# A graph-attention and slice-attention layer on one core: compact slice attention, shared PSUM places, and a new order of work at both ends

## The chip, the core and the metric

The kernel runs on one core of one Trainium2 chip. Its five engines work side by side: TensorE (PE, with its weight loads shown as PEld), VectorE (DVE), ScalarE (ACT), GpSimd (POOL) and SyncE (SP), which here issues transfers. The metric is device time in microseconds. The kernel before takes 2727.98 us, the median of three runs from 2726.14 to 2728.41; the profiled execution spans 2730.5 us.

## The reference

Everything is float32. `x` is 32 batches of 512 rows and 256 features; `adj` is a sparse 512 x 512 mask. Two layers with residuals follow each other, each on layer-normalised input:

```python
def _gat(inp, adj_mask, W, a):
    h = inp @ W
    f1, f2 = h @ a[:F, 0], h @ a[F:, 0]
    e = leaky_relu(f1[:, :, None] + f2[:, None, :], 0.2)
    if adj_mask is not None:
        e = where(adj_mask > 0, e, NEG_INF)
    return elu(einsum('bij,bjf->bif', softmax(e, axis=2), h))

# graph part
out = relu(x @ mlp1_w + mlp1_b)                       # 256 -> 512
out = elu(_gat(relu(out), None, W_fc, a_fc)) + out
out = relu(out @ mlp2_w + mlp2_b)                     # 512 -> 256
out = relu(elu(_gat(relu(out), adj, W_hand, a_hand)) + out)

# slice part: 8 heads, 64 slices, 64 features a head
fx = heads(x @ W_fx + b_fx);  xm = heads(x @ W_x + b_x)
w = softmax((xm @ W_slice + b_slice) / temp)          # rows x slices
token = (fx^T w) / (w.sum(rows) + 1e-5)
q, k, v = token @ W_q, token @ W_k, token @ W_v
out_slice = softmax(q k^T / 8) @ v
out = concat_heads(w @ out_slice) @ W_out + b_out

x = x + graph(layernorm(x));  x = x + slice(layernorm(x))
```

## The kernel before

A recorder takes down every engine instruction of all 32 batches, lets a scheduler of its own choose the order on each engine, and then emits them in that order. (So every instruction in the profile stands at one line, L262.) Each operation belongs to a batch (`age`) and a step; `TURNS` gives a step's turn relative to its batch, and `HEAD` and `TAIL` move whole batches at the two ends:

```python
PERIOD, SPARE = 91.1, 0.00
HEAD, TAIL = (-0.7, 1.6, 2.6), (0.1, -6.3, 142.4)
...
shift = dict(enumerate(HEAD)) | {last - i: s for i, s in enumerate(reversed(TAIL))}
...
keys[op] = (age - SAMPLE) * period + turn + shift.get(age, 0.0)
```

The steps of one batch, in the order of its data, with the names that the profile shows (a product of 256 or 512 columns in float32 appears as two TensorE instructions):

| step | TensorE's group in the profile | other work |
|---|---|---|
| norm1, mlp1 | mm<-xnT,w (512 columns) | layernorm, transposed through DRAM |
| h | mm<-wfc,o0T (257) | copies by ScalarE |
| factors, p | tr<-ident,sc; sm<-ident,fm | softmax factors, pT |
| pv | mm<-h,pT (257 and 256) | ELU of ELU, then u is flipped into u_stage |
| o1 | - | u_stage to DRAM and back as o1T, add o0T (VectorE) |
| mlp2, h2 | mm<-o1T,w (512); mm<-wh,o2T | |
| e, p2, pv2 | tr<-ident,h; mm<-h,p2T (257) | masked softmax, e through DRAM |
| norm2, w | mm<-weff,xn2T (512) | layernorm, softmax per head |
| sums, s1T | mm<-xn,w (257) | s1 through DRAM |
| tokens, att, vo, gg | mm<-s1T,wfx; mm<-nrow,bfx; mm<-tok,wqk; sm<-tok,qbd; tr<-ident,tokbd; tr<-ident,attbd; mm<-attT,tokg; mm<-wvo,meanbd | small attention over slices |
| out | mm<-gg,wT (256) | add x1, store |

Transposes go through DRAM in the inner batches and through TensorE (into PSUM) in the first and the last. PSUM has five places `mm`, two `tr` and one `sm`:

```python
def mm_tile(shape): return psum.tile(shape, F32, tag="mm", name="mm", bufs=5)
def tr_tile(shape): return psum.tile(shape, F32, tag="tr", name="tr", bufs=2)
def sm_tile(shape): return psum.tile(shape, F32, tag="sm", name="sm", bufs=1)
```

The way of u to mlp2, for inner batches:

```python
flip(u, stage[:, :, ts(i, Q)])                 # VectorE, four per batch
...
gather("u", stage, o1T)                        # four writes to DRAM, one read
for m in range(KH):
    nc.vector.tensor_tensor(o1, o1, swapped(o0T[:, m, :]), op=OP.add)
...
nc.tensor.matmul(pm..., w2[:, k, ts(m)], swapped(o1T[:, k, :]), ...)
```

The slice attention, with two heads on the diagonal of a 128 x 128 block:

```python
nc.tensor.matmul(pm[ts(s, C)], bfx[:, ts(s, C)], nrow[:, s], start=False, stop=True)  # 4 rows, 256 columns
...
nc.vector.tensor_copy(tok, pm)
for s in range(2):
    nc.gpsimd.tensor_copy(tokbd[ts(s, C), :, ts(s, G)], tok[ts(s, C), :, :])
...
for s in range(2):
    nc.scalar.activation(attbd[ts(s, G), :, ts(s, G)], sc[ts(s, G), :, :], AF.Exp, scale=C ** -0.5)
nc.vector.tensor_reduce(ra, attbd, axis=AX.X, op=OP.add)
nc.vector.reciprocal(ra, ra)
for p in range(NP):                            # NP = 4
    nc.tensor.transpose(pt[:, p, :], tokbd[:, p, :], ident)
nc.scalar.copy(tokg, pt)
for p in range(NP):
    nc.tensor.transpose(pt[:, p, :], attbd[:, p, :], ident)
diagonal(lambda s: attT..., lambda s: pt[ts(s, G), :, ts(s, G)])   # VectorE one half, ScalarE the other
...
nc.vector.scalar_tensor_tensor(gg[:, p, :], pg[:, s, :], ra[:, p : p + 1], bout, op0=OP.mult, op1=OP.add)
```

Of the kernel before, what the change touches and what calls it, by code (L numbers as in the profile page):

```python
# [13 lines left out]
ENGINES = ("tensor", "vector", "scalar", "gpsimd", "sync")  # L14

TURNS = {
    "load": -225.4, "norm1": -221.3, "mlp1": -189.8, "h": -116.6, "factors": -114.5,
    "p": -107.9, "pv": -95.7, "o1": -92.0, "mlp2": -64.3, "h2": -55.6, "e": -48.0,
    "p2": -45.0, "pv2": -16.2, "norm2": -4.3, "w": 49.4, "sums": 56.1, "s1T": 80.7,
    "tokens": 121.1, "att": 121.3, "vo": 145.5, "gg": 149.5, "out": 160.2,  # L20
}
PERIOD, SPARE = 91.1, 0.00

HEAD, TAIL = (-0.7, 1.6, 2.6), (0.1, -6.3, 142.4)


SAMPLE, SETUP = 8, 15.0
# [8 lines left out]
class Recorder:  # L36
# [190 lines left out]
    def order(self):  # L227


        steps, keys, ends = {}, {}, {}  # L230
        for op in self.ops:
            steps.setdefault((op.age, op.step), []).append(op)
        names = list(TURNS)
        for (age, step), ops in steps.items():
            at = TURNS.get(step, -1e5)
            till = TURNS[names[min(names.index(step) + 1, len(names) - 1)]] if age >= 0 else at
            costs = [op.cost if op.engine == "tensor" else 0.02 for op in ops]
            costs = [0.0 if op.joint else cost for op, cost in zip(ops, costs)]
            part = 0.0
            for op, cost in zip(ops, costs):  # L240
                keys[op] = age * PERIOD + at + part / sum(costs) * (till - at)
                part += cost
        for op in steps[-1, "setup"]:
            keys[op] = SETUP
        for op in self._schedule([op for op in self.ops if op.age < SAMPLE + 5], keys.get, SPARE):
            ends[op.age] = max(ends.get(op.age, 0.0), op.end)
        period = (ends[SAMPLE] - ends[SAMPLE - 4]) / 4
        starts = {step: [op.start for op in steps[SAMPLE, step]] for step in TURNS}
        last = max(age for age, _ in steps)
        shift = dict(enumerate(HEAD)) | {last - i: s for i, s in enumerate(reversed(TAIL))}  # L250
        for (age, step), ops in steps.items():
            for i, op in enumerate(ops):
                if age >= 0:
                    turn = starts[step][i * len(starts[step]) // len(ops)]
                    keys[op] = (age - SAMPLE) * period + turn + shift.get(age, 0.0)
                else:
                    keys[op] = -SAMPLE * period + SETUP if step else -1e5
        return self._schedule(self.ops, keys.get, SPARE)
# [40 lines left out]
def adj_ffn_kernel(  # L299
# [45 lines left out]
    def ts(i, n=P):  # L345
        return slice(i * n, (i + 1) * n)

    def new(name, shape, bufs=1, tag=None, dtype=F32):
        return sbuf.tile(list(shape), dtype, name=name, tag=tag or name, bufs=bufs)
# [2 lines left out]
        return psum.tile(shape, F32, tag="mm", name="mm", bufs=5)  # L352

    def tr_tile(shape):
        return psum.tile(shape, F32, tag="tr", name="tr", bufs=2)

    def sm_tile(shape):
        return psum.tile(shape, F32, tag="sm", name="sm", bufs=1)

    EDGES = (0, B - 1)  # L360
    Q = 32
# [5 lines left out]
    def by_dma(what, b):  # L367

        return what in FLIPPED and b not in EDGES
# [28 lines left out]
    def bcast_dram(ap, n):  # L398

        return bass.AP(tensor=ap.tensor, offset=ap.offset, ap=[[0, P], [1, n]])  # L400
# [4 lines left out]
    def load_x(b):  # L405
        if b < B:
            xt[b] = new("xt", [P, NT, D])
            nc.sync.dma_start(xt[b], x[b].rearrange("(p t) d -> p t d", p=P))

    ident = new("ident", [P, P])  # L410
    nc.gpsimd.memset(ident, 0.0)
    nc.gpsimd.affine_select(
# [38 lines left out]
    w2 = new("w2", [P, KH, D])  # L451
    nc.sync.dma_start(w2, mlp2_w.rearrange("(k p) f -> p k f", p=P))
    b2 = new("b2", [P, KD])
    nc.scalar.dma_start(b2, mlp2_b.rearrange("(m p) -> p m", p=P))

    wh = new("wh", [P, KD, D + 2])
    nc.sync.dma_start(wh[:, :, :D], W_hand.rearrange("(k p) f -> p k f", p=P))
    logits(a_hand, D)
    wfx = new("wfx", [P, KD, INNER])
    nc.scalar.dma_start(wfx, W_fx.rearrange("(k p) f -> p k f", p=P))  # L460
    bfx = new("bfx", [NP, P])
    nc.scalar.dma_start(bfx, b_fx.rearrange("(p f) -> p f", p=NP))

    bout = new("bout", [P, D])
    nc.sync.dma_start(bout, bcast_dram(b_out, D))
# [10 lines left out]
    nc.gpsimd.memset(qbd, 0.0)  # L476
    meanbd = new("meanbd", [P, NP, P])
    nc.gpsimd.memset(meanbd, 0.0)
    attbd = new("attbd", [P, NP, P])
    nc.gpsimd.memset(attbd, 0.0)  # L480


    mbias = new("mbias", [P, NT, N])
# [47 lines left out]
    wx = new("wx", [P, KD, INNER], tag="med", bufs=2)  # L531
    nc.sync.dma_start(wx, W_x.rearrange("(k p) f -> p k f", p=P))
    bxc = new("bxc", [P, NP])
    nc.scalar.dma_start(bxc, b_x.rearrange("(m p) -> p m", p=P))
    bsl = new("bsl", [P, G])
    nc.scalar.dma_start(bsl, bcast_dram(b_slice, G))
    for k in range(KD):
        pt = tr_tile([P, INNER])
        for p in range(NP):
# [28 lines left out]


    wo = new("wo", [P, NP, D], tag="med", bufs=2)  # L570
    nc.scalar.dma_start(wo, W_out.rearrange("(k p) f -> p k f", p=P))
    wv2T = twice_transposed(W_v)
    for p in range(NP):
        pv = mm_tile([P, D])
# [156 lines left out]
    def middle(b, o1T):  # L731
# [20 lines left out]
        f2b = tr_tile([P, N])  # L752
        for j in range(NT):
            nc.tensor.transpose(f2b[:, ts(j)], h[:, j, D + 1 : D + 2].to_broadcast([P, P]), ident)
        nc.step = "e"
        pT = new("p2T", [P, NT, N])
        if by_dma("e", b):
# [63 lines left out]
    def back(b, x1):  # L821
# [86 lines left out]

        pn = sm_tile([NP, P])
        nc.tensor.transpose(pn, s1[:, :, D], ident)  # L910
        nrow = new("nrow", [NP, 2, NP, G], tag="tokg")
        for s in range(2):
            nc.vector.tensor_tensor(
                nrow[:, s], ident[:NP, :NP, None].to_broadcast([NP, NP, G]),
                pn[:, None, ts(s, G)].to_broadcast([NP, NP, G]), op=OP.mult,
            )

        nc.step = "tokens"
# [3 lines left out]
        for p in range(NP):  # L922
            for k in range(KD):
                for s in range(2):
                    nc.tensor.matmul(
                        pm[ts(s, C), p, :].rearrange("c (a i) -> c a i", i=Q),
                        wfx[:, k, ts(2 * p + s, C)],
                        s1T[:, k, :].rearrange("p (a n i) -> p n a i", n=NP, i=Q)[:, p, ts(s, 2)],
                        start=(p == 0 and k == 0), stop=False,
                    )  # L930
        for s in range(2):
            nc.tensor.matmul(
                pm[ts(s, C)], bfx[:, ts(s, C)], nrow[:, s], start=False, stop=True
            )
        nc.joint = False

        def diagonal(dst, src):
# [2 lines left out]

        tok = new("tok", [P, NP, G])
        nc.vector.tensor_copy(tok, pm)
        for s in range(2):
            nc.gpsimd.tensor_copy(tokbd[ts(s, C), :, ts(s, G)], tok[ts(s, C), :, :])
        pq = mm_tile([P, NP, G])
        nc.tensor.matmul(pq, wqk, tok, start=True, stop=True)
        diagonal(lambda s: qbd[ts(s, C), :, ts(s, G)], lambda s: pq[ts(s, C), :, :])
# [7 lines left out]
        nc.vector.tensor_tensor(  # L955
            sc, psc, amax[:, :, None].to_broadcast([P, NP, G]), op=OP.subtract
        )
        for s in range(2):
            nc.scalar.activation(
                attbd[ts(s, G), :, ts(s, G)], sc[ts(s, G), :, :], AF.Exp, scale=C ** -0.5  # L960
            )
        ra = small("ra", [P, NP])
        nc.vector.tensor_reduce(ra, attbd, axis=AX.X, op=OP.add)
        nc.vector.reciprocal(ra, ra)
        nc.step = "vo"

        pt = tr_tile([P, NP, P])
        for p in range(NP):
            nc.tensor.transpose(pt[:, p, :], tokbd[:, p, :], ident)
        tokg = new("tokg", [P, NP, P])  # L970
        nc.scalar.copy(tokg, pt)
        pt = tr_tile([P, NP, P])
        for p in range(NP):
            nc.tensor.transpose(pt[:, p, :], attbd[:, p, :], ident)
        attT = new("attT", [P, NP, G])
        diagonal(lambda s: attT[ts(s, G), :, :], lambda s: pt[ts(s, G), :, ts(s, G)])
        pa = mm_tile([P, NP, G])
        for p in range(NP):
            nc.tensor.matmul(pa[:, p, :], tokg[:, p, :], attT[:, p, :], start=True, stop=True)
        diagonal(lambda s: meanbd[ts(s, C), :, ts(s, G)], lambda s: pa[ts(s, C), :, :])  # L980
        nc.step = "gg"
        gg = med("gg")
        for p2 in range(NP // 2):
            pg = mm_tile([P, 2, D])
            for s in range(2):
                p = 2 * p2 + s
                nc.tensor.matmul(pg[:, s, :], meanbd[:, p, :], wvo[:, p, :], start=True, stop=True)
            for s in range(2):
                p = 2 * p2 + s
                nc.vector.scalar_tensor_tensor(  # L990
                    gg[:, p, :], pg[:, s, :], ra[:, p : p + 1], bout, op0=OP.mult, op1=OP.add
                )
        nc.step = "out"
        for t2 in range(NT // 2):
            po = mm_tile([P, 2, D])
            for s in range(2):
                t = 2 * t2 + s
                for p in range(NP):
                    nc.tensor.matmul(
                        po[:, s, :], wT[:, p, ts(t)], gg[:, p, :],  # L1000
                        start=(p == 0), stop=(p == NP - 1),
                    )
            nc.vector.tensor_tensor(
                x1[:, ts(t2, 2), :], po, x1[:, ts(t2, 2), :], op=OP.add
            )
        nc.sync.dma_start(out[b].rearrange("(p t) d -> p t d", p=P), x1)

    for b in range(B):
        nc.age = b
# [58 lines left out]
```

## Time and profile before

| what | value |
|---|---|
| time, median of 3 | 2727.98 us |
| span of the profiled execution | 2730.5 us |
| instructions | 34562 |
| moved by DMA | 375.35 MB, mean 137 GB/s |
| q1 (issued by hardware queues) | 371.01 MB, 47.8% of 16 engines' span |
| mm<-wfc,o0T x2048 | 479.5 us busy |
| mm<-h,pT x2048 | 459.6 us busy |
| transposes of tokbd and attbd, 128 each | 20.6 and 19.8 us busy |

How to read it: a group's busy time counts overlapping instructions once, and matmuls overlap their neighbours, so the mean length of one (380 ns for 257 columns) is longer than the distance between two starts. Costs on TensorE are therefore better taken from starts in the order of time. A profile's view by stretches gives the busy time of each engine in chosen windows; the granted clock is the share of full speed that TensorE was given. In a list of waits each row names who waited, for whom, the sum, how often, and the longest.

### The profile page before, as it was taken

The page shows a single profiled execution, that of the slowest core. Times are in us where ns is not written, and L with a number is a line of the kernel's source. Part 1 is how long each engine was busy: PE and PEld are TensorE (multiplying, and loading weights), DVE is VectorE, ACT ScalarE, POOL GpSimd, SP SyncE. Part 2 cuts the span into 40 slices and gives each one's busy share as a digit, 9 for nine tenths or more (in the row PEclk, how much of TensorE's full clock was granted, in tenths as well). Part 3 has the DMA queues.
Part 4 walks back from the last instruction along what each step waited for, and adds up shares of the span by engine and source line. Part 5 has one row for each costly group of instructions (what it writes and reads, how often), then busy time and mean ns, then how long its engine had stood idle before and what let it go on. Part 6 is the DMA issues. An engine that isn't in the chain of part 4 may idle for free.

```text
span 2730.5 us, 34562 instructions
## 1 busy us (share of the span) xinstructions
PE 2655.7 (97%) x11965; PEld 1970.5 (72%) x11965; DVE 2096.8 (77%) x5190; ACT 1101.5 (40%) x2038; POOL 154.7 (6%) x234
## 2 busy tenths in 40 slices
PE   7999999999999999999999999999999999999886
PEld 5776677777777777777777777777777777677665
DVE  6577777887778887777887777887777887777854
ACT  2443443433444433344443444443444443444321
POOL 1000000000000000000000000000000000000000
PEclk9999999999999999999999999999999999999988
DMA  5125445554455555456545445645445545445420
GB/s 167 47 63 158 118 140 162 152 157 134 122 161 162 158 151 141 129 147 169 166 136 155 124 140 169 168 132 161 121 141 170 164 138 159 119 135 153 116 85 8
DMA packets 465078, 375.35 MB, mean 137 GB/s; under 512 B 86532, under 2 KB 382088, under 8 KB 464904
## 3 DMA queue, kind: packets, MB, share of 16 engines
q1 hardware_dynamic: 461568, 371.01, 47.8%
q10 hardware_dynamic: 3336, 2.14, 0.3%
q8 instruction: 95, 1.56, 0.2%
q14 instruction: 79, 0.65, 0.1%
HBM read 197.96 MB, written 175.11 MB: 137 GB/s over the span
## 4 chain that ended last, share of the span: by engine, by line
PE 69%; DVE 17%; DMA 8%; ACT 2%; issue 2%; SPq 1%; POOL 1%; DVEq 0%; ACTq 0%; POOLq 0%
PE mm L262 66%; DMA o1T<-scr 3%; DVE w L262 2%; PE tr L262 2%; DVE u L262 2%; DVE e L262 2%; DMA xt<-in_x_dram 2%; SPq L262 1%; DMA scr<-u_stage 1%; PE sm L262 1%; POOL ln_rstd L262 1%; DVE rs L262 1%; DVE e_stage L262 1%; DVE mx L262 1%; DVE u_stage L262 1%
## 5 line engine op out<-in xcount | busy, mean ns | idle before, releaser
L262 PE MATMUL mm<-wfc,o0T 128*128 128x257 f32 x2048 | 479.5, 380 | 0.0
L262 PE MATMUL mm<-h,pT 128*128 128x256 f32 (+1 forms) x2048 | 459.6, 380 | 2.1 <-DVE pT L262 1.5
L262 PEld LDWEIGHTS mm<-wfc,o0T 128*128 128x128 f32 x2048 | 381.4, 189 | 81.7 <-issue 32.5
L262 PEld LDWEIGHTS mm<-h,pT 128*128 128x128 f32 x2048 | 382.8, 189 | 64.2 <-DVE pT L262 4.9
L262 PE MATMUL mm<-xn,w 128*128 128x257 f32 x1024 | 264.4, 384 | 8.4 <-DVE w L262 4.3
L262 ACT COPY h<-mm 128x257 f32<-128x257 f32 (+1 forms) x384 | 143.2, 373 | 318.8 <-PE mm L262 311.0
L262 PE MATMUL mm<-gg,wT 128*128 128x256 f32 x1024 | 249.4, 380 | 0.0
L262 PE MATMUL mm<-xnT,w 128*128 128x512 f32 x512 | 244.7, 612 | 4.4 <-DMA xnT<-scr 2.5
L262 PE MATMUL mm<-o1T,w 128*128 128x512 f32 x512 | 230.3, 601 | 7.7 <-DVE o1T L262 7.5
L262 PE MATMUL mm<-h,p2T 128*128 128x257 f32 x1024 | 236.7, 382 | 0.7 <-ACT p2T L262 0.7
L262 PE MATMUL mm<-weff,xn2T 128*128 128x512 f32 x512 | 232.2, 594 | 0.2 <-ACT xn2T L262 0.2
L262 PEld LDWEIGHTS mm<-xn,w 128*128 128x128 f32 x1024 | 190.8, 192 | 36.6 <-issue 8.1
L262 PEld LDWEIGHTS mm<-h,p2T 128*128 128x128 f32 x1024 | 194.9, 191 | 30.0 <-ACT p2T L262 1.1
L262 PEld LDWEIGHTS mm<-gg,wT 128*128 128x128 f32 x1024 | 192.4, 191 | 29.4 <-issue 1.4
L262 ACT ACTIVATE u<-mm,rd 128x256 f32<-128x256 f32 x192 | 90.4, 472 | 263.3 <-DVE rd L262 191.5
L262 PEld LDWEIGHTS mm<-o1T,w 128*128 128x128 f32 x512 | 95.7, 191 | 123.1 <-issue 91.5
L262 DVE SCALAR_TENSOR_TENSOR e<-tr,h,mbias 128x512 f32<-128x512 f32 x128 | 92.4, 743 | 101.9 <-PE tr L262 101.9
L262 ACT ACTIVATE e<-e,nmax 128x512 f32<-128x512 f32 x128 | 92.4, 722 | 187.0 <-DVE nmax L262 186.0
L262 PEld LDWEIGHTS mm<-xnT,w 128*128 128x128 f32 x512 | 94.5, 195 | 99.5 <-issue 76.7
L262 DVE STREAM_TRANSPOSE o_stage<-o2T 128x512 f32<-128x512 f32 x64 | 45.5, 711 | 157.0 <-ACT o2T L262 157.0
L262 PEld LDWEIGHTS mm<-weff,xn2T 128*128 128x128 f32 x512 | 92.8, 191 | 90.3 <-issue 86.9
L262 ACT ACTIVATE m<-m 128x512 f32<-128x512 f32 x192 | 119.8, 625 | 78.6 <-DVE m L262 78.5
(150 smaller groups left out, 3938.8 us busy)
## 6 DMA issues: line engine op xcount, KB each, us to landing
scr<-xn_stage SPq DMA_DIRECT2D x240, 128.0 KB, 2.6
scr<-u_stage SPq DMA_DIRECT2D x120, 256.0 KB, 4.8
o1T<-scr SPq DMA_DIRECT2D x30, 1024.0 KB, 6.1
scr<-e_stage SPq DMA_DIRECT2D x120, 256.0 KB, 4.8
p2T<-scr SPq DMA_DIRECT2D x30, 1024.0 KB, 5.2
scr<-w_stage SPq DMA_DIRECT2D x120, 256.0 KB, 5.4
w_raw<-scr SPq DMA_DIRECT2D x30, 1024.0 KB, 5.9
xt<-in_x_dram SPq DMA_DIRECT2D x32, 512.0 KB, 4.6
```

What stands on the lines that cost most here:

```text
L262: getattr(getattr(self.nc, op.engine), op.method)(*op.args, **op.kwargs)
```

## The change

It has six parts.

1. **Compact slice attention.** The attention is no longer spread on the diagonal before it is transposed. Two pairs of heads lie side by side, so two transposes of 128 x 128 bring all of `tok`, and two all of `sc`, where four each were needed; the diagonal form of tok is made by the copies out of PSUM. The attention is normalised before the transpose, so gg needs only an add. The bias of the tokens is a product with 128 padded rows.
2. **Shared PSUM places.** `sm` is given up and `tr` has three places.
3. **f2b copied out** of PSUM by ScalarE in the first and the last batch, which frees its place.
4. **Turns.** Other base turns, and at both ends a shift for each step of the first three and the last three batches.
5. **Start.** ScalarE runs one small exp first, so that its table is loaded at once; x of batch 0 comes in two halves; weights' transfers b2, wfx, bfx, bxc, bsl and wo are issued by SyncE, and ScalarE keeps b1 and wfc.
6. **Last stores** of the last batch by tile, each after its own add.

The diff, cut to its core:

```diff
-PERIOD, SPARE = 91.1, 0.00
-HEAD, TAIL = (-0.7, 1.6, 2.6), (0.1, -6.3, 142.4)
+PERIOD, SPARE = 92.2, 0.00
+HEAD = (
+    (43, -22, -32, -121, -9, -3, -23, ...),
...
+shift = {(age, step): s for age, row in shift.items() for step, s in zip(TURNS, row)}
-keys[op] = (age - SAMPLE) * period + turn + shift.get(age, 0.0)
+keys[op] = (age - SAMPLE) * period + turn + shift.get((age, step), 0.0)
...
-        return psum.tile(shape, F32, tag="tr", name="tr", bufs=2)
+        return psum.tile(shape, F32, tag="tr", name="tr", bufs=3)
-        return psum.tile(shape, F32, tag="sm", name="sm", bufs=1)
+        return tr_tile(shape)
...
+            for t in range(0, NT, NT // 2 if b == 0 else NT):
+                nc.sync.dma_start(xt[b][:, t : t + n], rows[:, t : t + n])
+    warm = new("warm", [P, 1])
+    nc.vector.memset(warm, 0.0)
+    nc.scalar.activation(warm, warm, AF.Exp)
...
-    nc.scalar.dma_start(wfx, W_fx.rearrange("(k p) f -> p k f", p=P))
+    nc.sync.dma_start(wfx, W_fx.rearrange("(k p) f -> p k f", p=P))
...
+        if not by_dma("e", b):
+            pt, f2b = f2b, new("f2b", [P, N], tag="acb")
+            nc.scalar.copy(f2b, pt)
...
-            nc.tensor.matmul(
-                pm[ts(s, C)], bfx[:, ts(s, C)], nrow[:, s], start=False, stop=True
-            )
+                nc.tensor.matmul(
+                    pm[ts(s, C), a::2], bfx[:, ts(a, C)], nrow[:, s, a], start=False, stop=(a == 1)
+                )
...
-            nc.gpsimd.tensor_copy(tokbd[ts(s, C), :, ts(s, G)], tok[ts(s, C), :, :])
...
-            nc.scalar.activation(
-                attbd[ts(s, G), :, ts(s, G)], sc[ts(s, G), :, :], AF.Exp, scale=C ** -0.5
-            )
+        nc.scalar.activation(sc, sc, AF.Exp, scale=C ** -0.5)
-        nc.vector.tensor_reduce(ra, attbd, axis=AX.X, op=OP.add)
+        nc.vector.tensor_reduce(ra, sc, axis=AX.X, op=OP.add)
         nc.vector.reciprocal(ra, ra)
+        nc.vector.tensor_tensor(sc, sc, ra[:, :, None].to_broadcast([P, NP, G]), op=OP.mult)
...
-        for p in range(NP):
-            nc.tensor.transpose(pt[:, p, :], tokbd[:, p, :], ident)
-        nc.scalar.copy(tokg, pt)
+        for q in range(NP // 2):
+            nc.tensor.transpose(pt[:, ts(q, 2), :], tok[:, ts(q, 2), :], ident)
+        diagonal(lambda a: tokbd[ts(a, G), :, ts(a, C)], lambda a: pt[ts(a, G), :, :])
-        for p in range(NP):
-            nc.tensor.transpose(pt[:, p, :], attbd[:, p, :], ident)
-        diagonal(lambda s: attT[ts(s, G), :, :], lambda s: pt[ts(s, G), :, ts(s, G)])
+        for q in range(NP // 2):
+            nc.tensor.transpose(pt[:, ts(q, 2), :], sc[:, ts(q, 2), :], ident)
+        nc.scalar.copy(attT, pt)
...
-                nc.vector.scalar_tensor_tensor(
-                    gg[:, p, :], pg[:, s, :], ra[:, p : p + 1], bout, op0=OP.mult, op1=OP.add
-                )
+            nc.vector.tensor_tensor(
+                gg[:, ts(p2, 2), :], pg, bout[:, None, :].to_broadcast([P, 2, D]), op=OP.add
+            )
...
+            for s in range(2):
+                t = 2 * t2 + s
+                nc.vector.tensor_tensor(x1[:, t, :], po[:, s, :], x1[:, t, :], op=OP.add)
+                nc.sync.dma_start(rows[:, t, :], x1[:, t, :])
```

## The prediction

> **What bounds the kernel now.** I read the page's busy shares and slices first, then a table of busy time in chosen stretches, then TensorE's order of time inside one batch and in the drain, and last the list of waits.
>
> ```profile
> PE 2655.7 (97%) x11965; PEld 1970.5 (72%) x11965; DVE 2096.8 (77%) x5190; ACT 1101.5 (40%) x2038; POOL 154.7 (6%) x234
> ...
> PEclk9999999999999999999999999999999999999988
> ```
>
> ```profile
> 52.00:300.00 248.00, 243.15 (x1083) 179.85 (x1082) 167.96 (x408) 107.41 (x197) 9.95 (x16) 0.99 0.35 95
> ...
> 600.00:2300.00 1700.00, 1693.58 (x7673) 1260.71 (x7672) 1362.70 (x3364) 708.13 (x1314) 105.34 (x146) 1.00 0.52 148
> ...
> 2500.00:2647.00 147.00, 135.99 (x613) 99.20 (x612) 96.14 (x224) 46.15 (x87) 3.02 (x8) 0.95 0.40 114
> 2647.00:2731.00 84.00, 53.85 (x236) 38.55 (x234) 41.34 (x94) 18.27 (x33) 2.06 (x4) 0.81 0.03 13
> ```
>
> TensorE is the bound, busy 97%. The last four rows (stretch, length, busy time of PE, PEld, DVE, ACT, POOL, granted clock, DMA share, GB/s) say that the 1700 us in the middle have 6 us of idle left, while the last 84 us have 30 us of it and a granted clock of 0.81. So a gain comes either from fewer TensorE products per batch or from the two ends.
>
> Inside one batch, TensorE's order of time (start, length, group) is dense:
>
> ```profile
> 1509.84 1.15 PE L262 MATMUL mm<-s1T,wfx 128*64 128x64 f32 x32
> ...
> 1518.94 0.61 PE L262 MATMUL tr<-ident,tokbd 128*128 128x128 f32 x4
> 1519.39 1.02 PE L262 MATMUL mm<-xnT,w 128*128 128x512 f32 x2
> ...
> 1528.63 1.03 PE L262 MATMUL mm<-wfc,o0T 128*128 128x257 f32 x4
> 1529.50 7.03 PE L262 MATMUL mm<-o1T,w 128*128 128x512 f32 x16
> ```
>
> From starts I take costs: a transpose 0.11 us (four in 0.45), a 257-wide product (two instructions) 0.43, a 512-wide one 0.86. Starts of the o1T group from batch to batch: 15 periods between 1041.52 and 2264.13 make **81.5 us**; single periods go from 81.05 to 82.40. The difference is a wait just ahead of that group, and the list of waits names its source:
>
> ```profile
> DVE o1T L262 <- DMA o1T<-scr: 64.4, 28, 6.6
> ```
>
> In 28 batches VectorE sits idle, 2.3 us each, until the transfer that brings the transposed u back has landed; it then adds, and only then may mlp2 run.
>
> The drain, same columns, idle and its releaser in brackets:
>
> ```profile
> 2652.01 1.12 PE L262 MATMUL tr<-ident,e 128*128 128x128 f32 x4 [4.05 <-ACT e L262]
> 2654.42 1.12 PE L262 MATMUL tr<-ident,e 128*128 128x128 f32 x4 [1.30 <-ACT e L262]
> ...
> 2678.94 1.94 PE L262 MATMUL tr<-ident,xn 128*128 128x128 f32 x8 [8.60 <-DVE xn L262]
> ...
> 2718.44 7.81 PE L262 MATMUL mm<-gg,wT 128*128 128x256 f32 x32
> ```
>
> The last batch runs alone: each step of its chain leaves TensorE waiting for softmax, ELU, layernorm, with nothing of batch 30 left to fill in.
>
> **What the Trainium skill says.** "TensorE: Matmul & The Clock Gate", Part 1: after about 3.4 us idle the array is gated to half rate and gets the full rate back only after as long a busy stretch. The trace agrees: clock 0.81 in the drain, and the first 512-wide products, at 12.19 us, start 0.86 us per instruction apart, later 0.43. So a filled gap pays twice. Same page, Part 4: a transpose lands in PSUM and needs an engine to copy it out; here 276 ns each and then a ScalarE or VectorE copy of 0.37 to 0.59. "ScalarE: Activation LUTs", What ACT_TABLE_LOAD costs: 1283 ns for the load; the trace shows 1283, once. "DMA: Bandwidth & Descriptors", Issuing engines are not separate DMA queues: which engine issues saves only its issuing time; in the first 11 us ScalarE's queue shows issues of 0.39 to 1.67 us each, the table load behind them at 10.25.
>
> **The change part by part.**
>
> *Compact attention.* Per batch it drops four of the eight transposes: 4 x 0.11 = 0.44 us of TensorE, 14 us in 32 batches. The bias products become eight instructions 128 wide instead of four 256 wide: same columns, and the padding from 4 to 128 rows costs no columns; call it 0. Copies of attT: one ScalarE copy (0.37) for a VectorE one of 0.41 and a ScalarE one behind it. The softmax gains a multiply (about 0.42) and its reduce goes from 0.69 to about 0.42; gg goes from four of 0.48 to two of about 0.67. VectorE is at 77% and not the bound, so these count only in chains.
>
> **Does the 0.44 us reach the period?** All of it lies between the last P.V product and mlp2. In the batch shown that stretch is 1509.84 to 1529.50, 19.66 us. Counted in the changed order it holds 12 h products instead of 13 (-0.43), four transposes fewer (-0.44), one transpose of the sums' column more (+0.11), and some 0.3 less in waits for attT and between the narrow products: about 18.6. But what ends it is the transfer chain: last flip of u at 1515.40, read issued 1522.82, adds from 1528.48. The flips, the transfers and their order on the queue stay the same in the new order. So I expect the stretch to stay near 20 us, with a wait before mlp2 of about 1 us in place of the work removed. The h product moved out goes into the other part of the batch (+0.43, less 0.11). Net, 81.5 stays 81.5; I book 0.1 us less for 27 batches: **-3**.
>
> *Shared PSUM places.* No TensorE group in the steady batch waits for a place; 0 there. At the edges e's transposes come 2.4 us apart with one free place; a third place and f2b copied out (0.6 us more of ScalarE) let them come at VectorE's pace, three operations of 0.69 = 2.1. Contained in the drain below.
>
> *Start.* First transpose at 7.97, first mlp1 product at 12.19: the copies of xnT waited for ScalarE's table load (10.25 to 11.53). With the load at the head they can run when the transposes are there, near 9.2: -2.4. x(0) in two halves: at most 0.5. W_x's wait at 25 us (1.5) may go; the factors of batch 0 lose their filler of mlp1 products (three pairs, 2.5 us). Sum **-3**.
>
> *Filling, 52 to 600 us.* Idle there is 9 us, and two half-clock stretches cost some 5. New turns for batches 0 to 2 may take a little: **-2**.
>
> *Draining.* In the changed order the sums, slice attention and output products of batch 30 (about 6.9 + 5.9 + 6.9 = 20 us) lie inside the last batch's chain. From the weff products of batch 30 to the end I count 74 us of TensorE work at full clock. In the kernel before, the last 76 us of such work start at 2600, so this much takes 129 us. Walk of the changed order from there:
> - to the last batch's P.V: VectorE does the softmax of batch 30 first (2683.75 to 2697.2 in the trace for one batch, 13.4) plus its flips and two more (five of 0.65), from 1.9 us on, so e starts at 18.5, takes 8.3 and some 2 of other work, then exp, transpose, copy: P.V at 31;
> - P.V to the next transposes: 17.9 in the trace, some 2 longer with VectorE shared, 2 shorter at full clock: 49, products at 51;
> - weff to the s transposes' end: 21 in the trace; here 23.6, because the w transposes come after the output products of batch 30: 74.6;
> - slice attention and output: 2702.75 to 2726.25 in the trace, 23.5; 1.2 shorter with the compact form: with copies 97.6;
> - last add and store: 2726.28 to 2730.5, 4.2; by tile, a half-size add and a quarter of the bytes: about 3.2.
>
> That is 101 against 129: -28; I book **-26**, since in such walks some wait is always forgotten. Before it, 2500 to 2600 holds 7 us of idle; new turns: **-4**.
>
> Sum: -3 -3 -2 -26 -4 = -38, from 2727.98 to **2690**.
>
> **Rivals.**
> 1. *The transposes' time is real gain.* If the u chain came sooner (a quicker flip or read), 0.44 to 0.9 us per batch would count, 12 to 24 us, and the time would be 2666 to 2678. For it: the ready time scatters, in some batches no wait is seen. Against it: the 2.3 us of VectorE idle for that transfer.
> 2. *The new order makes a steady wait elsewhere.* The slice attention chain is now qk, max, subtract, exp, sum, reciprocal, multiply, transpose, and VectorE holds xn flips and the tokbd copy in between; the w tiles of the third and fourth row block are used within 0.5 us of their softmax. Half a microsecond per batch makes +14: 2704, more if several add up.
> 3. *The drain is bound by VectorE.* Batch 30's softmax sits ahead of e of batch 31. If fillers delay the last batch's chain as much as they fill, the drain gives only 10: 2706.
>
> **Range and chances.** The drain may give 12 to 34, the steady part -18 to +14 (it multiplies by 27), the start and filling 0 to 10. Not all at one end together: 2664 to 2712. Faster by over 2% needs under 2673.4, that is rival 1 with the full drain: 0.2. Slower by over 2% would need 2 us more per batch: 0.02.
>
> **What would show it.** Right: o1T group still 81.3 to 81.7 us apart, VectorE's idle for o1T's transfer larger than 64 us, waits of TensorE (or of its weight loads) on o1T up by 0.5 us or more per batch; first mlp1 product near 9.5 us; the last 101 us from batch 30's weff products, idle in the last 84 us down from 30 to under 20, clock above 0.81. Wrong: a period of 81.0 or less (rival 1); a new line of TensorE waits for sc, attT, qbd or w in some 27 batches (rival 2); a drain as long as before with VectorE near full in it (rival 3).

## The result

The changed kernel takes **2689.26 us** (median of 4 runs, 2687.21 to 2691.71) against 2727.44 for the kernel before: ratio 0.986, 95% interval 0.984 to 0.988. That is 38 us less, 1.4%.

Line 1 of the page and the row of the granted clock in 40 slices, changed kernel:

```profile
PE 2633.9 (98%) x11965; PEld 1969.6 (73%) x11965; DVE 2084.3 (77%) x5161; ACT 1090.6 (41%) x2009; POOL 90.9 (3%) x171
...
PEclk9999999999999999999999999999999999999998
```

TensorE still has 11965 instructions. Four transposes a batch less are made up by four bias products more.

The table by stretches (columns as in the prediction):

```profile
52.00:300.00 248.00, 242.81 (x1082) 179.82 (x1081) 171.68 (x416) 108.37 (x199) 7.57 (x12) 0.99 0.36 98
...
600.00:2300.00 1700.00, 1689.07 (x7682) 1262.53 (x7681) 1356.12 (x3349) 700.79 (x1291) 55.64 (x103) 1.00 0.53 148
...
2500.00:2606.00 106.00, 100.84 (x467) 76.11 (x466) 80.75 (x184) 40.38 (x74) 1.48 (x4) 0.99 0.39 107
2606.00:2690.00 84.00, 66.62 (x326) 50.82 (x325) 41.58 (x105) 17.91 (x35) 1.26 (x2) 0.80 0.13 41
```

The middle is nearly as before, with 11 us of TensorE idle instead of 6. The last 84 us hold 17 us of TensorE idle instead of 30, at a clock of 0.80 instead of 0.81.

Where the time went is read by laying the starts of the o1T group (the first mlp2 product of each batch) of both traces side by side:

| o1T group | before | changed | lead | gained in the stretch | predicted |
|---|---|---|---|---|---|
| batch 2 | 217.75 | 217.13 | 0.6 | 0.6 (start) | 3 |
| batch 6 | 552.23 | 542.04 | 10.2 | 9.6 (filling) | 2 |
| batch 27 | 2264.13 | 2252.32 | 11.8 | 1.6 (steady) | 3 |
| batch 29 | 2429.86 | 2415.87 | 14.0 | 2.2 | 0 |
| end | 2730.5 | 2689.9 | 40.6 | 26.6 (drain) | 30 |

The period is the same: 81.51 us before, 81.50 after, each over the 15 periods from batch 12 to batch 27. But the inside of a batch is not what the prediction said. TensorE's order of time from the last P.V product to mlp2:

```profile
1497.90 0.27 PE L276 MATMUL tr<-ident,s 128*4 128x128 f32 x1
1498.10 1.15 PE L276 MATMUL mm<-s1T,wfx 128*64 128x64 f32 x32
1499.13 0.43 PE L276 MATMUL mm<-nrow,bfx 128*64 128x128 f32 x2
1499.92 0.65 PE L276 MATMUL mm<-nrow,bfx 128*64 128x128 f32 x6 [0.36 <-DVE nrow L276]
...
1515.46 2.33 PE L276 MATMUL mm<-wfc,o0T 128*128 128x257 f32 x10
1517.63 4.88 PE L276 MATMUL mm<-o1T,w 128*128 128x512 f32 x11
```

No wait stands ahead of the o1T group here. The time is in the eight bias products: from 1499.13 to 1500.50, 1.37 us, where the four before took 0.58. The row of sums is now transposed after P.V and not inside it, so VectorE's nrow comes late. The same is in the changed kernel's list of waits (who waited, for whom, sum, times, longest):

```profile
PEld mm L276 <- DVE nrow L276: 17.2, 28, 1.0
PEld mm L276 <- DVE o1T L276: 12.2, 43, 1.0
...
DVE o1T L276 <- DMA o1T<-scr: 11.4, 14, 1.6
```

VectorE's wait for the transfer of o1T fell from 64.4 us to 11.4. In the median batch its add ended 0.06 us before the first mlp2 product began; now it ends 0.62 us before. What stands in the place of the removed transposes is therefore, in most batches, **TensorE's own work and its wait for nrow**. VectorE itself starts the add of o1T right behind the adds of gg, without idle:

```profile
1515.66 0.69 DVE L276 TENSOR_TENSOR gg<-mm,bout 128x512 f32<-128x512 f32 x1 [0.17 <-PE mm L276]
1516.27 1.88 DVE L276 TENSOR_TENSOR o1T<-o1T,o0T 128x512 f32<-128x512 f32 x3
```

So the add's start no longer shows when the transfer landed. In the trace the landings of batches 10 to 26 scatter from 12.5 to 14.6 us after the last flip of u. In five of these 17 batches the add ends only 0.10 us ahead, and there the transfer still ends the stretch.

### The profile page after: what moved, and what is told of

Read it like the earlier page. It is cut to its first block, busy times and chain, and to the rows that moved or that the text cites. A ratio compares the mean times of both kernels' runs of the same rounds, so it can differ in the third digit from the quotient of the medians.

```text
span 2689.9 us, 34228 instructions
## 1 busy us (share of the span) xinstructions
PE 2633.9 (98%) x11965; PEld 1969.6 (73%) x11965; DVE 2084.3 (77%) x5161; ACT 1090.6 (41%) x2009; POOL 90.9 (3%) x171
## 3 DMA queue, kind: packets, MB, share of 16 engines
q8 instruction: 95, 1.56, 0.2%
## 4 chain that ended last, share of the span: by engine, by line
PE 72%; DVE 19%; DMA 5%; ACT 2%; issue 1%; SPq 1%; POOL 0%; DVEq 0%; ACTq 0%
PE mm L276 69%; DVE u L276 4%; PE tr L276 3%; DMA scr<-s_stage 2%; DVE pT L276 2%; DMA s1T<-scr 1%; DVE u_stage L276 1%; DVE m L276 1%; DVE xn_stage L276 1%; DVE ln_st L276 1%; DVE x L276 1%; SPq L276 1%; DVE s L276 1%; DVE s_stage L276 1%; DVE w L276 1%
## 5 line engine op out<-in xcount | busy, mean ns | idle before, releaser
L276 PE MATMUL mm<-wfc,o0T 128*128 128x257 f32 x2048 | 474.0, 380 | 0.0
L276 PE MATMUL mm<-xnT,w 128*128 128x512 f32 x512 | 256.8, 610 | 0.5 <-ACT xnT L276 0.5
L276 PE MATMUL mm<-xn,w 128*128 128x257 f32 x1024 | 251.8, 383 | 2.3 <-DVE rs L276 1.0
L276 PE MATMUL mm<-gg,wT 128*128 128x256 f32 x1024 | 234.2, 380 | 0.0
L276 PEld LDWEIGHTS mm<-xn,w 128*128 128x128 f32 x1024 | 185.3, 191 | 36.9 <-issue 3.2
L276 DVE SCALAR_TENSOR_TENSOR e<-tr,h,mbias 128x512 f32<-128x512 f32 x120 | 86.5, 742 | 98.3 <-PE tr L276 98.3
L276 ACT ACTIVATE m<-m,neg 128x512 f32<-128x512 f32 x192 | 137.9, 718 | 4.3
L276 ACT ACTIVATE w<-w 128x512 f32<-128x512 f32 x128 | 79.8, 630 | 135.7 <-DVE w L276 134.3
```

What stands on the lines that cost most here:

```text
L276: getattr(getattr(self.nc, op.engine), op.method)(*op.args, **op.kwargs)
```

## The experiments

Two theories of the steady part were open. **T1**, from the prediction: the transfers of o1 end the stretch from pv to mlp2, and less TensorE work turns into waiting. **T2**, from the trace: TensorE's work and small waits fill it, and less work is less time. For the ends: is it the new order, the compact attention, or the places and stores? "Stretch" below is from the start of the last P.V product to the first mlp2 product; shortest values and medians are of batches 10 to 26, the mean period is that from batch 12 to batch 26.

| kernel | time, us | period, shortest / mean | stretch, shortest / median | add ends ahead, median |
|---|---|---|---|---|
| before | 2727.44 | 81.05 / 81.49 | 19.96 / 20.29 | 0.06 |
| changed | 2689.26 | 81.25 / 81.51 | 19.94 / 19.95 | 0.62 |
| 1 compact alone | 2770.28 | 82.82 / 82.96 | 22.17 / 22.17 | 1.13 |
| 2 turns alone | 2838.43 | 85.43 / 85.70 | 20.23 / 20.23 | 0.46 |
| 5 no bias | 2687.01 | 80.60 / 81.02 | 19.29 / 19.33 | 0.27 |
| 6 row early | 2739.85 | 81.18 / 81.62 | 19.35 / 19.58 | 0.10 |
| 7 bias on 4 rows | 2690.97 | 81.26 / 81.57 | 19.95 / 19.96 | 0.57 |
| 9 transposes twice | 2697.00 | 81.70 / 81.71 | 20.39 / 20.39 | 0.68 |
| 10 row early, order kept | 2694.44 | 81.11 / 81.81 | 19.69 / 20.21 | 0.10 |
| 12 row early, statistics late | 2696.56 | 81.59 / 81.69 | 20.17 / 20.18 | 0.59 |

### 1. The compact attention alone, in the kernel before

```diff
-        pt = tr_tile([P, NP, P])
-        for p in range(NP):
-            nc.tensor.transpose(pt[:, p, :], tokbd[:, p, :], ident)
+        pt = tr_tile([P, NP, C])
+        for q in range(NP // 2):
+            nc.tensor.transpose(pt[:, ts(q, 2), :], tok[:, ts(q, 2), :], ident)
 (and the rest of the slice attention; TURNS, HEAD, TAIL as before)
```

> The kernel before with the compact slice attention alone (bias products included); order, starting and draining shifts, PSUM places and stores as before. Theory A (the steady stretch from pv to mlp2 can't be shortened by taking transposes away, and the saving lies in start, filling and drain): period from one o1T add to the next 81.3 to 81.8 us, time 2718 to 2735 us. Theory B (the eight 128-wide transposes and the block-diagonal copies are a real gain of TensorE time, hidden in the changed kernel by its new order): period at most 81.0 us, time at most 2712 us.

Measured: 2770.28 us, ratio 1.016 (1.014 to 1.017), slower. Both theories missed. The scheduler sets the changed operations among the old turns in a new order, and the steady list of TensorE's waits (600 to 2300 us) has a new first row:

```profile
PE mm L262 <- DVE nrow L262: 28.2, 21, 1.3
```

That is 1.3 us in each of 21 batches. The add of o1T ends 1.13 us ahead in the median batch, so the transfers rarely hold this kernel. The stretch grew by 2 us although its work shrank.

### 2. The new turns alone, in the kernel before

```diff
-PERIOD, SPARE = 91.1, 0.00
+PERIOD, SPARE = 92.2, 0.00
-HEAD, TAIL = (-0.7, 1.6, 2.6), (0.1, -6.3, 142.4)
+HEAD = ((43, -22, -32, ...), ...)   # and TAIL, TURNS, shifts by step
```

> The kernel before with the new turns alone: the new table of turns, the period given to the scheduler, the shifts by step at both ends. Attention, PSUM places, table load and stores as before. Theory A (the shifts by step are what saves time): 2684 to 2700 us, period 81.3 to 81.8 us. Theory B (the shifts fit only together with the compact attention and the shared places): over 2715 us.

Measured: 2838.43 us, ratio 1.040 (1.039 to 1.042), slower: theory B, and by more than it said. The steady list shows three waits of 1.0 to 1.4 us that neither kernel has:

```profile
PE mm L276 <- DVE rs L276: 26.4, 19, 1.4
PE mm L276 <- DVE rd L276: 23.5, 19, 1.2
PE mm L276 <- DVE tok L276: 20.1, 20, 1.0
```

They make 3.5 us a batch, near the 4.2 by which the mean period grew. Attention alone and turns alone each make the kernel slower; the whole change makes it faster. The table of turns fits one list of operations only.

### 3 and 4. The old shift at one end

```diff
 3: -HEAD = ((43, -22, -32, ...), ...)
    +HEAD = tuple((s,) * 22 for s in (-0.7, 1.6, 2.6))
 4: -TAIL = ((0, 0, 0, 0, -27, ...), ...)
    +TAIL = tuple((s,) * 22 for s in (0.1, -6.3, 142.4))
```

> The changed kernel with one shift for every step in batches 0 to 2, as the kernel before had it; all else as changed. Theory A (by the leads of the two traces, about 12 us of the 38 were won before 600 us): 2697 to 2703 us, and the lead at the fifth o1T add is gone. Theory B (as the prediction's sum had it, start and filling are worth 5 us): 2692 to 2696 us. In both the time from the last weff to the end stays 110 us.

> The changed kernel with one shift for every step in the last three batches, as the kernel before had it; all else as changed. Theory A (by the leads of the two traces the drain won about 27 us, by its order): 2710 to 2722 us, and from the last weff to the end 125 to 135 us instead of 110. Theory B (the compact attention and the stores by tile win the drain, whatever its order): 2692 to 2705 us.

Measured for 3: 2763.58 us, ratio 1.013 (1.012 to 1.015). It loses 73 us before batch 3's o1T group (371.1 instead of 298.2) and then runs as the changed kernel does. Its row between the o1T groups of batches 2 and 3:

```profile
254.00:371.00 117.00, 88.51 (x355) 65.64 (x355) 66.45 (x161) 31.89 (x60) 3.19 (x5) 0.84 0.36 99
```

28 us idle, at clock 0.84. So this does not measure what the new shifts won over the old kernel: beside the new turns the old shift is simply wrong. Both theories missed. From the last weff to the end it stayed at 109 us, as both said.

Measured for 4: 2713.83 us, ratio 0.995 (0.994 to 0.997): theory A, 24.6 us above the changed kernel. Its table of the last stretch:

```profile
2628.00:2711.80 83.80, 56.09 (x255) 41.33 (x253) 39.32 (x93) 17.47 (x31) 1.26 (x2) 0.82 0.03 13
```

28 us idle again, and 139 us from batch 30's weff to the end instead of 110 (before: 143). This kernel has the compact attention, the places and the stores by tile, so these alone don't shorten the drain. But the shifts by step alone don't either: run 2 has them without the rest, needs 138 us from batch 30's weff, and has 26 us idle in its last 84:

```profile
2752.00:2836.20 84.20, 58.29 (x258) 43.01 (x256) 38.13 (x89) 16.71 (x30) 2.05 (x4) 0.82 0.03 13
```

The drain is shortened by **the shifts by step, together with the operations that they were tuned for**. As in 3, an old shift beside new turns may do harm of its own, so 24.6 us is no clean measure of the gain. No run takes out the places, the f2b copy or the stores by tile alone.

### 5. No bias products

```diff
-        pn = sm_tile([NP, P])
-        nc.tensor.transpose(pn, s1[:, :, D], ident)
-        (two tensor_tensor into nrow)
...
-        for a in range(2):
-            for s in range(2):
-                nc.tensor.matmul(pm[ts(s, C), a::2], bfx[:, ts(a, C)], nrow[:, s, a], ...)
```

It leaves b_fx out of the computation.

> The changed kernel without the bias products of the token slices, the row of sums and its transpose (b_fx is left out of the computation; it is zero in these inputs). This takes 9 TensorE instructions and their waits, about 1.6 us a batch, out of the stretch from pv to mlp2. Theory A (the transfers of o1 bound that stretch: 5.5 us to the last flip, 13.1 us for both transfers, 0.75 us for the add make 19.3 us): the period falls by 0.3 to 0.7 us, TensorE's wait on o1T grows to 0.7 us a batch or more, and the time is 2668 to 2682 us. Theory B (TensorE's own work and small waits fill the stretch): the period falls by 1.2 us or more, to 80.3 us or less, time at most 2655 us. Theory C (the scheduler's new order loses what is taken away): 2684 us or more.

Measured: 2687.01 us, ratio 0.986 (0.984 to 0.987). The period went as theory A said: about 1.6 us of work and waits taken out, 0.49 us of mean period gained. But the limit that it named is not what stopped the shortest batches. In TensorE's steady list (600 to 2300 us) a wait for tok has taken the place of the one for nrow, and the wait on o1T is small. VectorE's wait for the transfer comes back too:

```profile
PE mm L276 <- DVE tok L276: 22.4, 20, 2.0
PE mm L276 <- DVE o1T L276: 1.7, 2, 1.3
```

```profile
DVE o1T L276 <- DMA o1T<-scr: 19.2, 22, 2.8
```

In most of the shortest batches TensorE doesn't wait for o1T at all: the add ends 0.27 us or more ahead. So the 19.3 us of the shortest stretch are TensorE's work and a wait of 1.1 us for tok. That theory A's sum also makes 19.3 is a coincidence. The late transfers show in the mean, which lies 0.42 us above the shortest period (changed kernel: 0.26).

The time missed theory A's range: at batch 28's o1T group it leads the changed kernel by 13 us, and from there, in another order, it needs 362.7 us to the end against 356.2. The rest, 6.6 us between the profiled spans (2683.3 us here), is 2.3 us between the medians.

### 6. The row of sums earlier, by the scheduler

```diff
+        nc.step = "sums"
         pn = sm_tile([NP, P])
         nc.tensor.transpose(pn, s1[:, :, D], ident)
         (two tensor_tensor into nrow)
         nc.step = "s1T"
```

> The changed kernel with the transpose of the row of sums and its spread (nrow) recorded in the step of the sums instead of the step of the tokens, so that they come before pv, as they ran in the kernel before. The work is the same. Theory A (the waits for nrow, 0.36 to 0.9 us a batch in the stretch from pv to mlp2, cost their own time): period 80.6 to 81.2 us, time 2665 to 2682 us. Theory B (the stretch is bound by the transfers, which leave under 0.7 us): period 81.3 to 81.6 us, the wait taken over by o1T, time 2685 to 2692 us.

Measured: 2739.85 us, ratio 1.005 (1.003 to 1.006), slower. The steady part went as theory B said (mean period 81.62, the add of o1T 0.10 ahead instead of 0.62). Between the profiled spans it is 44 us slower: 16 by batch 2's o1T group, 8 from there to batch 28's, and 21 after that. A changed step turned the whole order about.

### 7. The bias products on 4 rows

```diff
-    pm[ts(s, C), a::2], bfx[:, ts(a, C)], nrow[:, s, a], start=False, stop=(a == 1)
+    pm[ts(s, C), a::2], bfx[:NP, ts(a, C)], nrow[:NP, s, a], start=False, stop=(a == 1)
```

> The changed kernel with the bias products on their 4 rows that hold anything, instead of on 128 rows of which 124 are zero. The eight products and their columns are the same. Theory A (rows cost TensorE nothing): a product of 64 columns takes the same time within 10 ns, period and time the same (2685 to 2693 us). Theory B (padding was put there because a product on 4 rows takes longer beside products on 128): the eight take 0.3 us a batch more or over, time 2694 us or more.

Measured: 2690.97 us, ratio 0.987 (0.986 to 0.989): theory A. The order of time shows the same two pieces, now with 4 rows:

```profile
1502.14 0.43 PE L276 MATMUL mm<-nrow,bfx 4*64 4x128 f32 x2
1502.88 0.65 PE L276 MATMUL mm<-nrow,bfx 4*64 4x128 f32 x6 [0.32 <-DVE nrow L276]
```

0.43 and 0.65 us, as with 128 rows. The padding costs nothing; the late nrow costs the time.

### 8. The scheduler told of later landings

```diff
-    ISSUE, BEGIN, LAND, BEHIND = 0.45, 1.2, 0.9, 2.7
+    ISSUE, BEGIN, LAND, BEHIND = 0.45, 1.2, 1.5, 2.7
```

> The changed kernel with the scheduler told that a transfer lands 0.6 us later than it thinks (1.5 us after its bytes instead of 0.9). The work is the same; only the order may differ. Theory A (the add of o1T ends 0.68 us before TensorE wants it, and nothing waits on it): the order round mlp2 shifts by one instruction or two, period 81.2 to 81.8 us, time 2684 to 2697 us. Theory B (rarely waiting batches are those where the transfers come late, and the order hides it once it knows): period 80.9 us or less, time 2680 us or less.

Measured: 4091.19 us, ratio 1.500 (1.497 to 1.503). Both theories missed. With one number of its model changed, the scheduler orders the batches nearly one behind another: 122.4 us a batch in the mean, TensorE busy 77%. It says nothing of o1T; it shows how near the tuned order lies to bad ones.

After these, the experiments keep the changed kernel's order of instructions and edit only what is emitted.

### 9. The four transposes done twice, order kept

```diff
         for op in self.order():
-            getattr(getattr(self.nc, op.engine), op.method)(*op.args, **op.kwargs)
+            for _ in range(2 if op.mark == "twice" else 1):
+                getattr(getattr(self.nc, op.engine), op.method)(*op.args, **op.kwargs)
```

> The changed kernel in its own order, with each of the four 128-wide transposes of tokens and attention done twice in a row (the second writes the same values to the same place), so that there are eight, as in the kernel before. That adds 4 times 0.11 us of TensorE a batch between pv and mlp2. Theory A (in the changed kernel TensorE's own work fills that stretch; the add of o1T ends 0.6 us before it is wanted): period 81.8 to 82.0 us, time 2699 to 2706 us. Theory B (as the prediction had it, the transfers end the stretch): o1T takes up the 0.44 us, period 81.3 to 81.6 us, time 2688 to 2693 us.

Measured: 2697.00 us, ratio 0.989 (0.988 to 0.991), 7.7 us above the changed kernel: between the theories. The doubled transposes in the order of time:

```profile
1511.74 0.38 PE L277 MATMUL tr<-ident,tok 128*128 128x128 f32 x2
...
1512.82 0.38 PE L277 MATMUL tr<-ident,tok 128*128 128x128 f32 x2
...
1514.34 0.60 PE L277 MATMUL tr<-ident,sc 128*128 128x128 f32 x4
```

The shortest period rises by 0.45 us, all of the 4 x 0.11. The mean rises by only 0.20, and 81.71 is nearly the shortest now: the batches in which the transfer came late had room for it. So the transposes that the change removed are worth about 8 us in this order, neither 0 nor 14.

### 10. The row of sums earlier, order kept

The transpose goes 32 TensorE instructions ahead, and nrow behind it, in batches 3 to 27.

```diff
+            for op in row:
+                order.remove(op)
+            order[at:at] = row[:1]     # 32 TensorE instructions earlier
+            ...
+            order[at:at] = row[1:]     # nrow, 4 TensorE instructions behind it
```

> The changed kernel in its own order, with one thing moved in batches 3 to 27: the transpose of the row of sums runs 32 TensorE instructions earlier, inside pv, and the two VectorE instructions of nrow follow it. No other instruction changes its place. Theory A (the waits for nrow and the slow products round them cost their own time): eight bias products in 0.6 us instead of 1.4, the stretch from pv to mlp2 at 19.3 to 19.6 us instead of 19.95, where the add of o1T stops it, period 80.7 to 81.1 us, time 2674 to 2683 us. Theory B (the time is taken up elsewhere in the batch, since the transpose must be done anyway and tok comes no earlier): period 81.3 us or more, time 2686 us or more.

Measured: 2694.44 us, ratio 0.988 (0.986 to 0.990): theory B, and a mean period 0.3 us longer. Order of time, then the lists of waits:

```profile
1508.33 0.61 PE L296 MATMUL mm<-nrow,bfx 128*64 128x128 f32 x8
1509.63 2.81 PE L296 MATMUL mm<-xnT,w 128*128 128x512 f32 x6 [0.69 <-DMA xnT<-scr]
```

```profile
PE mm L296 <- DMA xnT<-scr: 12.9, 16, 1.4
...
DVE o1T L296 <- DMA o1T<-scr: 22.9, 24, 3.2
```

The eight bias products take 0.61 us, as hoped. But VectorE has almost no idle (0.16 us) between 1489 us and the last flip of u. The 0.73 us of nrow, put in ahead of the flips of xn, push those flips back, and so the transfer of xnT. And they bring the last flip of u no sooner: it ends 5.8 us after the last P.V product starts, against 5.46. The waits for xnT and o1T took what nrow gave.

### 11. The first x in one piece, order kept

```diff
+            if op.mark == "whole":
+                op.args = self.whole      # (xt[0], rows)
+            if op.mark != "skip":
                 getattr(getattr(self.nc, op.engine), op.method)(*op.args, **op.kwargs)
```

> The changed kernel in its own order, with the first x in one transfer instead of two halves (the one stands where the first half stood). Theory A (the second half lands later than the whole did, 5.8 against 4.3 us, and it holds back the first mlp1 product): the first mlp1 product at 10.0 to 10.7 us instead of 11.19, the first o1T product and the time 0.5 to 1.5 us earlier. Theory B (the halves start the statistics earlier and are worth it): the first mlp1 product at 11.2 us or later. A difference of 1 us in the whole time is under what the runs resolve; it is read from the trace.

Measured: 2688.97 us, ratio 0.986 (0.984 to 0.988). The first mlp1 product starts at 10.54 us: theory A by its first mark. In the ten traces with halves it starts at 10.88 to 11.19, so the halves cost 0.3 to 0.65 us. By batch 2's o1T group (217.25 against 217.13) nothing of it is left.

### 12. Both moves, order kept

```diff
+            ln = [op for op in order[pv[-1] - BACK : pv[-1]]
+                  if op.engine == "vector" and op.step == "norm2"]
+            (taken out, and put in again behind the last flip of u)
```

The row is moved as in 10, but nrow stands behind the flips of xn.

> The changed kernel in its own order with two things moved in batches 3 to 27: the row of sums as in the run before (its transpose 32 TensorE instructions earlier, nrow behind the flips of xn), and the two statistics and four aggregates of the second layer norm that stood in VectorE's queue ahead of the last flips of u put behind the last of them (1.1 us of VectorE). The work is the same. Theory A (the stretch from pv to mlp2 has two limits of nearly the same length: TensorE's own work and its waits for nrow, 19.95 us, and the chain of VectorE's queue, flips, two transfers and add, 19.3 to 19.7 us; moving the row shortens only the first, both moves shorten both): last flip 4.7 to 5.2 us after the last pv product starts instead of 5.46, stretch 18.8 to 19.4 us at its shortest, period 80.6 to 81.1 us, time 2665 to 2681 us. Theory B (the transfers themselves vary by over 1 us and the later second layer norm is wanted as early as it was): period 81.3 us or more, time 2685 us or more.

Measured: 2696.56 us, ratio 0.989 (0.987 to 0.991): theory B by the time, but not for its reason. The wait on nrow is gone, o1T is ready 0.59 us ahead, and the list of waits has a new first row:

```profile
PE tr L305 <- ACT qbd L305: 26.0, 26, 1.1
```

The statistics now stand just ahead of the first copy of qbd in VectorE's queue, and TensorE waits 1 us in each of 26 batches for it. The last flip stayed at 5.46 us. The period is 0.18 us longer than the changed kernel's, though steadier: 81.59 to 81.75 in most batches. No reordering here beats the changed kernel beyond the scatter of the runs.

## Why the prediction was right, point by point

**The total** (2690 against 2689.26) is right, but a miss of under 1 us is luck. The parts are right in sign, and their errors cancel: filling gave 7.6 us more than booked; start, steady part and drain gave 2.4, 1.4 and 3.4 less, and batches 28 and 29 gave 2.2 that the sum didn't have.

**Steady part: right number, wrong mechanism.** The failed step is that the transfer chain ends the stretch, "with a wait before mlp2 of about 1 us in place of the work removed". The waits fell instead: VectorE's for the transfer from 64.4 us to 11.4 in all, TensorE's on o1T from 7.5 to 1.6. What took the place were the bias products, booked with "call it 0". They took 1.37 us instead of 0.58, through the wait on nrow. Columns and rows were counted rightly (7); the dependence was not. From the first s1T product to mlp2 the prediction counted about 18.6 us of TensorE's time. It took 19.53, and 0.79 of the difference are the bias products.

T1 is not all false. The landing scatters, and in about a third of the batches it still ends the stretch; mostly through these the mean period lies 0.26 us above the shortest. With 0.44 us put in (9), the gap closes to 0.01, and nearly half of the 0.44 reaches the mean. So the stretch has two limits that lie close: TensorE's work and its wait for nrow, 19.95 us in nearly every batch, and flips (5.46), transfers (12.5 to 14.6) and the first add (0.7), which make 18.7 to 20.8. Taking from one alone gives at most the distance to the other.

That the transposes gave about 8 us and the late nrow took them back is worked out from 9 and from the two bias times, and not shown: no run put the old bias products into the changed order. Runs 5, 10 and 12 took the wait for nrow away, and each time another wait behind VectorE's queue (tok, xnT's flips, qbd) took up much of the gain or more.

**Rivals.** Rival 1 is half true: real time, of which a kernel at two limits keeps half. Rival 2 came true on nrow, which it didn't name, and only to the amount that the transposes saved. Rival 3 did not come, though VectorE was nearly full (23.5 of 25 us) from batch 30's weff on, as the walk had it.

**Start.** The "first mlp1 product near 9.5 us" came at 11.19. Two terms were mis-sized. The halves were to give up to 0.5 and cost 0.3 to 0.65 (11). And the copies of xnT could not run near 9.2, since the eight transposes alone take 1.97 us; with x whole they start at 9.90, the product at 10.54. The table load at 1.21 us is out of the way, as said, and the wait of W_x's transposes is gone. Batch 0's o1T group is 3.7 us earlier (72.06 against 75.78), but batch 1's is 1.6 later, and at batch 2's 0.6 us of the lead is left.

**Filling** was booked at 2 and gave 9.6. About 5 of it lies between the o1T groups of batches 4 and 5. Rows of this stretch, first of the kernel before, then of the changed one:

```profile
384.17:471.28 87.11, 84.35 (x368) 61.77 (x369) 67.62 (x168) 34.30 (x63) 4.30 (x7) 0.96 0.50 139
```

```profile
378.90:460.70 81.80, 81.03 (x370) 60.43 (x368) 64.59 (x161) 34.04 (x63) 2.71 (x5) 1.00 0.53 148
```

In the kernel before, two waits near 450 us (tok 1.30, xnT 1.42) were followed by a clock of 0.96 in this stretch; the changed kernel keeps 1.00. I had seen the drops and booked only part of them. That these waits caused the drop is argued from their place only, and since run 3 measures something else, the cause of the other 5 us of filling stays open.

**Drain.** The step "101 us from batch 30's weff" was 110. TensorE's order of time there:

```profile
2579.69 7.03 PE L276 MATMUL mm<-weff,xn2T 128*128 128x512 f32 x16
...
2609.95 9.67 PE L276 MATMUL mm<-h,p2T 128*128 128x257 f32 x32 [0.46 <-ACT p2T L276]
...
2624.16 0.70 PE L276 MATMUL mm<-tok,wqk 128*128 128x256 f32 x2 [3.02 <-DVE tok L276]
...
2629.72 0.69 PE L276 MATMUL tr<-ident,xn 128*128 128x128 f32 x2 [1.56 <-DVE xn L276]
...
2634.35 2.02 PE L276 MATMUL mm<-weff,xn2T 128*128 128x512 f32 x2
...
2645.24 1.89 PE L276 MATMUL mm<-gg,wT 128*128 128x256 f32 x8
...
2660.92 1.25 PE L276 MATMUL tr<-ident,s 128*128 128x128 f32 x9
```

The walk held to P.V (30.3 us, 31 said) and to the next transposes (50.0, 49 said). It lost 8 of its 9 us on "products at 51" and on the 23.6 us from weff to the end of the s transposes: the products began at 54.7, and the end came at 82.5. Between lie batch 30's slice attention and a row of the table by stretches at half clock:

```profile
2625.20:2638.90 13.70, 11.36 (x37) 8.47 (x38) 5.41 (x18) 2.57 (x7) 1.26 (x2) 0.50 0.00 0
```

"Clock above 0.81" did not come: 0.80. The filling work has waits of its own (tok 3.02, xn 1.56), and a gap costs its own time and then a stretch at half clock. The prediction took over from the Trainium skill's "TensorE: Matmul & The Clock Gate", Part 1, that the half rate comes after about 3.4 us idle. Here less was enough. These are the 3.41 us ahead of each of the three drops to 0.50:

```profile
2601.32:2604.73 3.41, 0.80 (x6) 0.42 (x4) 3.23 (x6) 1.79 (x3) 0.00 (x0) 1.00 0.93 223
2621.79:2625.20 3.41, 0.70 (x2) 0.30 (x2) 3.24 (x8) 0.77 (x2) 0.00 (x0) 1.00 0.00 0
2666.18:2669.59 3.41, 1.28 (x10) 1.14 (x10) 1.64 (x4) 1.09 (x3) 0.00 (x0) 1.00 0.00 0
```

TensorE was busy 0.70 to 1.28 us of each, and none of its waits was longer than 3.02 us. So batch 30's work inside the last batch's chain fills the gaps, but a half-filled gap did not keep the clock.

On the other side, the stretch up to batch 30's weff gained more than the 4 booked: 129 less 110 is 19 of the 26.6, which leaves about 8. With the old shift at the end (4) the drain's gain is nearly all lost, and with the shift alone (2) it doesn't come, so it rests on the new order of the new operations. That it works through batch 30's work inside the last batch's chain is read from the order of time (its gg products at 2645.24 stand among the last batch's); no run moves that work alone.

## What to carry to other kernels

When two chains end a stretch within half a microsecond of each other, count both, and expect a saving on one to stop at the other; a list of waits names only the one that came last. A transfer that nobody is seen waiting for may still land late: look at its landing, not at the start of the work that uses it. A change that keeps the work but moves a small producer (here a transpose of 4 columns and its copy) later can cost as much as the work it saves. Where a scheduler orders the program, test a part with the emitted order held fixed: re-running it after edits of a line or two moved the time by 50 us (6) and by 1400 (8).

## What the runs showed of the hardware that was not expected

- A product of 128 columns on 4 rows took the same time as on 128 rows: six in 0.65 us either way (7).
- Half-clock stretches of 10.2 and 13.7 us in the drain hold TensorE busy for 7.4 and 11.4 us: a busy engine with short gaps stayed at 0.50.
- The 3.41 us ahead of a drop to half clock need not be idle: TensorE was busy for 0.70 to 1.28 us of them in the drain of the changed kernel, and for 1.40 us ahead of the drop at 450.06 us in the kernel before.
- The read that brings o1T back (1 MB) took from 5.5 to 7.7 us from issue to landing in batches 11 to 26 of the changed kernel, with the same instructions round it:

```profile
DMA to landing us min/median/max: 5.5/6.1/7.7
```
